# Branch taps as matmuls, one load per scan tile and step-size additions on ScalarE, in a four-layer kernel on one Trainium2 core

## The chip, the core and the metric

The kernel runs on one core of one Trainium2 chip, in one launch for a batch of eight images. The metric is the device time in microseconds (us), from the first to the last instruction and what little lies around them. All arithmetic is in 32-bit floats. The names of the engines in the profile are PE for TensorE (with PEld for its weight loads), DVE for VectorE, ACT for ScalarE, POOL for GpSimd, and SP for the engine that issues most of the DMAs; SPq and ACTq are the instruction queues of SP and ScalarE.

## The reference

Each image has 256 channels of 32 x 32 pixels, read as 1024 tokens. Four layers follow each other, each with a residual: attention over tokens, two 3x3 convolutions, and a large layer with a state-space scan ("mamba") on four groups of 64 channels, a gate, depthwise convolutions, a second attention and a projection. The change is in the scan of the last layer. Cut to that:

```
def mamba(xs, inw, convw, convb, xpw, dtw, dtb, alog, dp, outw):   # xs: tokens x 64
    xz = xs @ inw.T                                  # inw: 256 x 64
    u, z = jnp.split(xz, 2, axis=-1)                 # 128 channels each
    uc = causal depthwise convolution of u, 4 taps (convw), + convb
    u = silu(uc)
    xdbc = u @ xpw.T                                 # 4 + 16 + 16 columns
    dt = softplus(xdbc[..., :4] @ dtw.T + dtb)       # the step size
    Bm, Cm = xdbc[..., 4:20], xdbc[..., 20:]
    # scan over tokens, 128 channels x 16 states:
    #   h = exp(dt * A) * h + dt * u * Bm ;  y = sum over states of h * Cm
    y = selective_scan(u, dt, Bm, Cm, -exp(alog), dp)
    return y * silu(z) @ outw.T
```

## The kernel before

The program is written image by image, but it is not issued in that order. A recorder (class Plan) takes down every operation of all eight images, and a planner (arrange, L526) then writes the order of each engine by hand: it goes forward in time with a cost for each operation (cost, L329; matmul groups in appraise), and gives each engine the operation that can begin first. Among those that can begin equally soon it takes the one with the earliest due time. Due times come from the table PACE (L38): for every part and image four marks, between which the part's operations are spread. Only their order counts. The parts are A (first attention), O (its output projection), C (the two 3x3 convolutions), N (layer norm ahead of the scan), F0 to F3 (front of a branch), S (scan steps), Z0 to Z3 (back of a branch), B (gate, depthwise convolutions, second attention), E (the end), W and V (weights made once). The issue goes through one helper, so every line of the profile says L252; groups are told apart by tiles.

Each engine works off its order strictly one after another. So do the queues that issue DMAs: nearly all go through SP, and the weight chunks (chunk, L835; a ring of six tiles) through ScalarE's queue.

For every image there are four branches i, one for each group of 64 channels. branch_front (L1555) makes the scan's inputs:

- A matmul of 64 rows (the branch's channels in xn) by 128 columns (minw) into a two-bank PSUM tile, in two halves of 512 tokens; ScalarE copies the result into the single tile raw (L928), whose first three columns are zero.
- The four taps: ScalarE writes tap 3 with its bias into u, and VectorE adds the other three with three multiply-adds over 1024 columns. Tanh and one more VectorE step complete the silu. raw serves as scratch for the Tanh and again below.
- A small matmul makes Bm and Cm (low), which go to DRAM (bc). A second one makes the step size: VectorE adds dtb out of PSUM into a, ScalarE takes Abs and Exp, VectorE adds 1 into dt, and so on to the softplus. The step size dt and the product dt * u go to DRAM by store (L1547), ordered by channel group.

The scan (scan_steps, L1650) works on tiles of 128 partitions: 32 channels times four states. A scan tile therefore needs each row of dt and of dt * u four times (once for each state), and each row of bc 32 times. load_groups (L1665) and load (L1678) fetch these from DRAM with four DMAs each, one for every block of 32 partitions. For each of 64 units per image GpSimd multiplies (drive), and then twice ScalarE makes the decay into the only tile da in PSUM (decays) and VectorE scans (scan); VectorE multiplies by Cm (weigh), and TensorE sums over the four states with the 0/1 matrix sel (add_up, tile y). branch_back (L1625) uses the other 128 columns of minw for z.

conv_weights (L1406) prepares the weights of the two convolutions once, through the tiles room.

Of the kernel before, what the change touches and what calls it, by code (L numbers as in the profile page):

```python
# [20 lines left out]
P = 128  # L21
C = 256
# [17 lines left out]
        (-885, -784, -577, -524),  # L40
        (-103, -9, 78, 165),
        (485, 530, 588, 646),
        (870, 961, 1046, 1134),
        (1361, 1446, 1533, 1630),
        (1845, 1935, 2025, 2115),
        (2349, 2396, 2443, 2519),
        (2831, 2902, 2980, 3061),
    ),
    "B": (
        (1114, 1200, 1279, 1370),  # L50
        (1602, 1687, 1773, 1860),
        (2084, 2169, 2259, 2351),
        (2463, 2638, 2720, 2739),
        (3101, 3188, 3272, 3307),
        (3516, 3600, 3754, 3767),
        (3880, 3975, 4004, 4059),
        (4777, 4790, 5023, 5024),
    ),
    "C": (
        (-333, -53, 12, 184),  # L60
        (148, 323, 511, 689),
        (675, 782, 934, 1087),
        (1131, 1297, 1470, 1642),
        (1616, 1787, 1960, 2133),
        (2074, 2247, 2420, 2622),
        (2612, 2799, 2955, 3121),
        (3457, 3546, 3602, 3664),
    ),
    "E": (
        (1389, 1406, 1424, 1444),  # L70
        (1880, 1893, 2032, 2032),
        (2333, 2372, 2389, 2427),
        (2831, 2831, 2839, 2842),
        (3542, 3564, 3565, 3565),
        (3488, 3498, 3544, 3628),
        (3933, 3940, 3941, 4070),
        (4578, 4972, 4989, 5061),
    ),
    "F0": (
        (-559, -519, -387, -348),  # L80
        (363, 550, 550, 626),
        (1092, 1176, 1318, 1318),
        (1446, 1454, 1454, 1491),
        (1237, 1661, 1789, 1916),
        (1606, 1682, 1917, 1917),
        (2318, 2416, 2610, 2836),
        (2309, 2375, 2375, 2615),
    ),
    "F1": (
        (473, 510, 515, 531),  # L90
        (841, 1007, 1007, 1018),
        (1453, 1469, 1469, 1476),
        (1926, 2012, 2021, 2060),
        (2383, 2407, 2505, 2505),
        (2847, 2866, 2883, 2973),
        (2445, 2541, 2639, 2965),
        (3743, 3846, 3846, 3888),
    ),
    "F2": (
        (427, 665, 686, 726),  # L100
        (1098, 1110, 1122, 1137),
        (1591, 1596, 1608, 1621),
        (2148, 2148, 2150, 2159),
        (2673, 2691, 2758, 2758),
        (3061, 3062, 3062, 3067),
        (3456, 3471, 3476, 3483),
        (4079, 4079, 4079, 4079),
    ),
    "F3": (
        (741, 760, 761, 883),  # L110
        (1181, 1206, 1250, 1253),
        (1668, 1730, 1762, 1864),
        (2176, 2194, 2334, 2357),
        (2659, 2674, 2674, 2796),
        (3135, 3167, 3185, 3358),
        (3545, 3624, 3666, 3742),
        (4203, 4242, 4242, 4331),
    ),
    "N": (
        (228, 275, 297, 518),  # L120
        (894, 898, 916, 935),
        (1370, 1378, 1387, 1393),
        (1775, 1779, 1956, 1956),
        (2364, 2372, 2383, 2485),
        (2769, 2858, 2905, 2913),
        (3516, 3516, 3516, 3516),
        (3916, 3931, 3947, 3957),
    ),
    "O": (
        (-408, -360, -360, -222),  # L130
        (251, 266, 272, 304),
        (647, 699, 699, 717),
        (1141, 1144, 1164, 1169),
        (1628, 1641, 1641, 1653),
        (2121, 2128, 2128, 2130),
        (2664, 2673, 2673, 2673),
        (2983, 2987, 3029, 3137),
    ),
    "S": (
        (496, 662, 820, 969),  # L140
        (980, 1123, 1258, 1397),
        (1470, 1636, 1790, 1956),
        (1967, 2133, 2291, 2453),
        (2458, 2615, 2760, 2911),
        (2907, 3037, 3231, 3382),
        (3371, 3581, 3774, 3909),
        (3655, 3674, 4444, 4470),
    ),
    "V": (
        (-2135, -1874, -1869, -1869),  # L150
    ),
    "Z0": (
        (571, 587, 605, 700),
        (1086, 1087, 1087, 1125),
        (1562, 1567, 1573, 1651),
        (2046, 2046, 2067, 2274),
        (1457, 1941, 1964, 2015),
        (2915, 2931, 2940, 3087),
        (2942, 2968, 2993, 3076),
        (3891, 4014, 4213, 4213),  # L160
    ),
    "Z1": (
        (747, 752, 1035, 1038),
        (1215, 1215, 1215, 1325),
        (1653, 1666, 1667, 1787),
        (2101, 2105, 2228, 2271),
        (2632, 2641, 2641, 2719),
        (3117, 3172, 3218, 3304),
        (3106, 3600, 3605, 3608),
        (4127, 4151, 4151, 4159),  # L170
    ),
    "Z2": (
        (822, 833, 857, 967),
        (1360, 1394, 1403, 1429),
        (1878, 1878, 1905, 1931),
        (2340, 2377, 2377, 2392),
        (2686, 2778, 2788, 2829),
        (3276, 3276, 3399, 3482),
        (3695, 3695, 3735, 3945),
        (4495, 4548, 4753, 4758),  # L180
    ),
    "Z3": (
        (930, 938, 958, 959),
        (1442, 1444, 1445, 1457),
        (1878, 1881, 1882, 1883),
        (2411, 2421, 2447, 2452),
        (2890, 2903, 2904, 2905),
# [2140 lines left out]
```

## Time and profile before

| what | value |
| --- | --- |
| median of three runs | 5733.31 us (5718.4 to 5734.21) |
| the profiled execution | 5719.45 us, of which the span of its instructions is 5717.7 us |
| mean granted clock of TensorE in it | 0.898 of full speed |
| DMA moved | 553.96 MB, 97 GB/s on average |
| DMA issues for scan tiles (bc, dt, du) | 1024 + 512 + 512, each 128 KB |

The profile's groups show for each kind of instruction the engine, the tiles (out<-in, with buffer numbers left out), the shape, the count, then the busy time in us and the mean duration of one in ns, and last the idle time of the engine ahead of them with what ended it. A 512-column matmul of 32-bit floats appears as two records: the code issues 128 of them with minw, and the profile counts 256. In the table by stretches each row gives the length, then for each engine the busy time and number of instructions, then the granted clock of TensorE (PEclk), the share of DMA engines' time in use, and GB/s. Every number in this text that is called a share of the chain comes from the view that follows the work back from the last instruction.

### The profile page before, as it was taken

The page shows a single profiled execution, that of the slowest core. Times are in us where ns is not written, and L with a number is a line of the kernel's source. Part 1 is how long each engine was busy: PE and PEld are TensorE (multiplying, and loading weights), DVE is VectorE, ACT ScalarE, POOL GpSimd, SP SyncE. Part 2 cuts the span into 40 slices and gives each one's busy share as a digit, 9 for nine tenths or more (in the row PEclk, how much of TensorE's full clock was granted, in tenths as well). Part 3 has the DMA queues.
Part 4 walks back from the last instruction along what each step waited for, and adds up shares of the span by engine and source line. Part 5 has one row for each costly group of instructions (what it writes and reads, how often), then busy time and mean ns, then how long its engine had stood idle before and what let it go on. Part 6 is the DMA issues. An engine that isn't in the chain of part 4 may idle for free.

```text
span 5717.7 us, 56860 instructions
## 1 busy us (share of the span) xinstructions
PE 4851.9 (85%) x18854; PEld 1945.2 (34%) x18854; DVE 4044.5 (71%) x5285; ACT 2843.0 (50%) x3737; POOL 1309.9 (23%) x527
## 2 busy tenths in 40 slices
PE   8899898789799989999888998889889388587495
PEld 2343533432334333333333332333325033232132
DVE  3333667878866887687767686688866888688823
ACT  4343453456455646564555445465464345455242
POOL 0000123323320323112231123213240324133300
PEclk9999998899898999999899998889989589798597
DMA  3112434434342444324333334324433344233210
GB/s 121 55 55 74 127 84 127 130 99 116 110 120 65 122 120 125 87 79 124 111 96 92 96 98 115 85 78 121 120 101 91 89 127 117 60 112 109 60 34 23
DMA packets 267279, 553.96 MB, mean 97 GB/s; under 512 B 70616, under 2 KB 93784, under 8 KB 266976
## 3 DMA queue, kind: packets, MB, share of 16 engines
q1 hardware_dynamic: 182880, 413.89, 25.5%
q10 hardware_dynamic: 84096, 136.35, 8.2%
q8 instruction: 151, 2.47, 0.2%
q14 instruction: 152, 1.25, 0.1%
HBM read 478.98 MB, written 62.65 MB: 95 GB/s over the span
## 4 chain that ended last, share of the span: by engine, by line
PE 52%; DVE 22%; issue 9%; ACT 8%; DMA 7%; SPq 1%; POOL 1%; ACTq 0%; DVEq 0%; POOLq 0%
PE big L252 29%; PE cv L252 10%; PE acc L252 10%; DVE hs L252 10%; ACT p L252 3%; PE y L252 2%; DVE room L252 2%; ACT da L252 2%; DVE u L252 2%; DMA dt_m<-dt 1%; DMA du_m<-a 1%; DMA dt<-dt_m 1%; DVE fd L252 1%; SPq L252 1%; DMA bc<-bc 1%
## 5 line engine op out<-in xcount | busy, mean ns | idle before, releaser
L252 POOL TENSOR_TENSOR hs<-du,bc 128x1024 f32<-128x1024 f32 x512 | 1307.0, 2570 | 4069.7 <-PE y L252 1880.9
L252 ACT ACTIVATE p<-big 128x1024 f32<-128x1024 f32 x1024 | 1014.1, 1020 | 597.1 <-PE big L252 479.8
L252 ACT ACTIVATE da<-dt,a_neg 128x512 f32<-128x512 f32 x1024 | 708.0, 691 | 1044.8 <-DVE hs L252 814.8
L252 PE MATMUL acc<-p,v 128*64 128x512 f32 x3072 | 844.7, 634 | 82.1 <-ACT p L252 80.0
L252 PE MATMUL cv<-taps,w 128*128 128x256 f32 x3072 | 780.9, 405 | 90.2 <-DVE xt L252 30.4
L252 DVE TENSOR_TENSOR_SCAN hs<-da,carry,hs 128x512 f32<-128x512 f32 x512 | 653.6, 1276 | 199.1 <-ACT da L252 183.7
L252 DVE TENSOR_TENSOR_SCAN hs<-da,hs 128x512 f32<-128x512 f32 x512 | 623.2, 1217 | 236.6 <-ACT da L252 163.7
L252 DVE TENSOR_TENSOR hs<-hs,bc 128x1024 f32<-128x1024 f32 x512 | 725.9, 1421 | 64.3 <-ACT carry L252 59.4
L252 PEld LDWEIGHTS cv<-taps,w 128*128 128x128 f32 x3072 | 596.3, 201 | 367.6 <-issue 177.3
L252 PE MATMUL big<-q,k 64*128 64x512 f32 x2048 | 590.7, 652 | 40.5 <-ACT p L252 24.4
L252 DVE TENSOR_TENSOR p<-p 128x1024 f32<-128x1024 f32 x256 | 331.3, 1296 | 325.4 <-ACT p L252 194.1
L252 PE MATMUL y<-hs,sel 128*32 128x512 f32 x2048 | 372.6, 666 | 189.9 <-DVE hs L252 188.1
L252 PEld LDWEIGHTS acc<-p,v 128*64 128x64 f32 x3072 | 162.5, 138 | 671.5 <-issue 376.0
L252 PE MATMUL big<-qk,qk 32*128 32x512 f32 x2048 | 339.5, 691 | 36.7 <-DVE z L252 9.1
L252 PEld LDWEIGHTS big<-q,k 64*128 64x128 f32 x2048 | 161.3, 189 | 414.9 <-issue 215.4
L252 PE MATMUL cv<-p,v 128*64 128x512 f32 x1024 | 287.9, 640 | 3.2 <-DVE xt L252 3.2
L252 PE MATMUL big<-xn,w 128*128 128x512 f32 x512 | 231.4, 603 | 0.7 <-issue 0.6
L252 PE MATMUL big<-o,w 128*128 128x512 f32 x384 | 190.0, 644 | 44.0 <-DVE o L252 24.3
L252 PEld LDWEIGHTS y<-hs,sel 128*32 128x32 f32 x2048 | 54.9, 112 | 436.1 <-DVE hs L252 279.2
L252 PEld LDWEIGHTS big<-qk,qk 32*128 32x128 f32 x2048 | 93.3, 196 | 265.0 <-issue 169.5
L252 DVE SCALAR_TENSOR_TENSOR room<-room,vec,room 128x992 f32<-128x992 f32 (+1 forms) x128 | 165.5, 1293 | 12.7 <-ACT room L252 11.3
L252 PE MATMUL big<-fd,w 128*128 128x512 f32 x256 | 135.3, 681 | 43.6 <-DVE fd L252 31.9
(232 smaller groups left out, 5256.1 us busy)
## 6 DMA issues: line engine op xcount, KB each, us to landing
bc<-bc SPq DMA_DIRECT2D x1024, 128.0 KB
w<-wc ACTq DMA_DIRECT2D x384, 256.0 KB
dt<-dt_m SPq DMA_DIRECT2D x512, 128.0 KB
du<-du_m SPq DMA_DIRECT2D x512, 128.0 KB
rs<-inv SPq DMA_DIRECT2D x64, 256.0 KB
dt_m<-dt SPq DMA_DIRECT2D x64, 256.0 KB
du_m<-a SPq DMA_DIRECT2D x64, 256.0 KB
w<-in_wqk ACTq DMA_DIRECT2D x64, 128.0 KB
```

The costliest lines, as they stand in the source:

```text
L252: made = op["call"](*args, **kwargs).ins
```

## The change

Seven edits are made together:

1. The four taps go into the projection's weights. front_weights makes, once, four scaled copies of each branch's 64 x 128 weights (one for each tap), transposes them on TensorE and stores them in DRAM as two 128-row matrices per branch (wu). In branch_front two DMAs put the branch's 64 rows of xn twice into raw, into partitions 64 to 127 one column later than into 0 to 63, and four 512-column matmuls of 128 rows (two per half, accumulating) give the result of all four taps. ScalarE moves it from PSUM to u with the bias. The copy into raw and the three multiply-adds are gone.
2. The weights wu are fetched as a chunk for each branch, in the ring of six; minw keeps only the columns for z.
3. A scan tile's partitions are ordered by channel first and state second (sel, by_state), and dt, dt * u and bc are each loaded by one DMA of 128 partitions instead of four of 32.
4. The two additions of the step size (dtb, and 1) are Identity activations on ScalarE, no longer VectorE instructions.
5. All due times in PACE are new.
6. region (the planner's view of an access) counts several partition dimensions; the cost of a large memset is raised from 0.3 to 0.83 ns an element.
7. front_weights runs as the last piece of part V.

```diff
--- before.py
+++ after.py
@@ -37,167 +37,167 @@
 PACE = {
...
     "C": (
...
-        (2612, 2799, 2955, 3121),
-        (3457, 3546, 3602, 3664),
...
+        (3483, 3656, 3824, 3986),
+        (4157, 4407, 4623, 4825),
     ),
...
     "S": (
...
-        (3371, 3581, 3774, 3909),
-        (3655, 3674, 4444, 4470),
...
+        (4582, 4689, 4769, 4839),
+        (5152, 5207, 5207, 5581),
     ),
     "V": (
-        (-2135, -1874, -1869, -1869),
+        (306, 325, 327, 412),
     ),
...
@@ -297,8 +297,8 @@
         return a.tensor.name, 0, 1, a.offset, a.offset + sum((n - 1) * s for s, n in ap)
     row = int(np.prod(a.tensor.shape[1:]))
     p, at = divmod(a.offset, row)
-    end = p + (ap[0][1] - 1) * max(1, ap[0][0] // row) + 1
-    return a.tensor.name, p, end, at, at + sum((n - 1) * s for s, n in ap[1:])
+    end = p + sum((n - 1) * (s // row) for s, n in ap if s >= row) + 1
+    return a.tensor.name, p, end, at, at + sum((n - 1) * s for s, n in ap if s < row)
 
 
 def whole_banks(r):
@@ -344,7 +344,7 @@
         return (334 if e == 2 else 420), first
     if e == 1:
         if name == "memset":
-            took = 60 + 0.3 * n
+            took = 60 + (0.83 if n > P else 0.3) * n
         elif name == "tensor_tensor_scan":
             took = 70 + 2.3 * n
         elif name == "reciprocal":
@@ -858,9 +858,17 @@
     make_identity(nc, ident)
 
     sel = wp.tile([P, 32], F32, name="sel")
-    for s in range(4):
-        rows = slice(s * 32, s * 32 + 32)
-        vector.tensor_copy(sel[rows], ident[rows, rows])
+    pool.memset(sel, 1.0)
+    for base, sign in ((0, 1), (3, -1)):
+        pool.affine_select(
+            out=sel,
+            in_=sel,
+            compare_op=ALU.is_ge,
+            fill=0.0,
+            base=base,
+            pattern=[[-4 * sign, 32]],
+            channel_multiplier=sign,
+        )
 
     gmat = wp.tile([P, P], F32, name="gmat")
     pool.memset(gmat, 0.125)
@@ -905,6 +913,7 @@
     made_w = {"fcw": fc_w}
     for name in ("wc1", "wc2"):
         made_w[name] = wdp.tile([12, P, 4, P], F32, tag=name, name=name)
+    made_w["wu"] = wdp.tile([NB, P, 2, P], F32, tag="wu", name="wu")
     minus_s1 = wp.tile([P, 2], F32, name="minus_s1")
     vector.tensor_scalar_mul(minus_s1, vec[:, cols["s1"] : cols["s1"] + 2], -1.0)
     q_b = wp.tile([P, 2], F32, name="q_b")
@@ -1427,6 +1436,32 @@
             for k in range(2):
                 sync.dma_start(out=outer_w[:, :, k], in_=w[:, :, 2 * k])
 
+    def front_weights():
+
+        w = room[0][:, 0:C].rearrange("p (i n) -> p i n", i=NB)
+        sync.dma_start(out=w, in_=I["wu"])
+        scaled = room[2].rearrange("p (i k n) -> p i k n", i=NB, k=4)
+        ps = big_tile()
+        for i in range(NB):
+            for k in range(4):
+                vector.tensor_scalar(
+                    scaled[:, i, k], w[:, i], col("convw", 4 * i + 3 - k), None, ALU.mult
+                )
+            for k in range(2):
+                at = (2 * i + k) * P
+                tensor.matmul(
+                    ps[:, at : at + P],
+                    room[2][:, at : at + P],
+                    ident,
+                    start=True,
+                    stop=True,
+                )
+        vector.tensor_copy(room[2], ps)
+        sync.dma_start(
+            out=made_w["wu"].rearrange("i p k n -> p i (k n)"),
+            in_=room[2].rearrange("p (i n) -> p i n", i=NB),
+        )
+
     def transform(xt, stats, h):
 
         scale, shift = stats
@@ -1556,29 +1591,21 @@
 
 
         j, rows = i // 2, slice((i % 2) * 64, (i % 2) * 64 + 64)
-        ps = big_tile()
+        for half, at in ((slice(0, 64), 2), (slice(64, P), 3)):
+            sync.dma_start(out=raw[half, at : at + N], in_=inner(xn[j])[rows])
+        w, ps = chunk("wu", i), big_tile()
         for h in range(2):
-            tensor.matmul(
-                ps[:, HALVES[h]],
-                minw[rows, j, 0:P],
-                inner(xn[j])[rows, HALVES[h]],
-                start=True,
-                stop=True,
-            )
-        scalar.copy(raw[:, 3 : 3 + N], ps)
+            for k in range(2):
+                tensor.matmul(
+                    ps[:, HALVES[h]],
+                    w[:, k],
+                    raw[:, 2 - 2 * k + h * HALF : 2 - 2 * k + (h + 1) * HALF],
+                    start=k == 0,
+                    stop=k == 1,
+                )
         u = mp.tile([P, N], F32, tag="u", name="u", bufs=2)
         uu = u[:, 0:N]
-        scalar.activation(
-            uu,
-            raw[:, 3 : 3 + N],
-            AF.Identity,
-            bias=col("convb", i),
-            scale=col("convw", 4 * i + 3),
-        )
-        for k in range(3):
-            vector.scalar_tensor_tensor(
-                uu, raw[:, k : k + N], col("convw", 4 * i + k), uu, ALU.mult, ALU.add
-            )
+        scalar.activation(uu, ps, AF.Identity, bias=col("convb", i))
         th = raw[:, 3 : 3 + N]
         scalar.activation(th, uu, AF.Tanh, scale=0.5)
         vector.scalar_tensor_tensor(uu, th, 1.0, uu, ALU.add, ALU.mult)
@@ -1610,10 +1637,10 @@
             tensor.matmul(
                 ps[:, HALVES[h]], mdtw[:, i], u[:, HALVES[h]], start=True, stop=True
             )
-        vector.tensor_scalar_add(aa, ps, col("dtb", i))
+        scalar.activation(aa, ps, AF.Identity, bias=col("dtb", i))
         scalar.activation(ee, aa, AF.Abs)
         scalar.activation(ee, ee, AF.Exp, scale=-1.0)
-        vector.tensor_scalar_add(dd, ee, 1.0)
+        scalar.activation(dd, ee, AF.Identity, bias=ones[:, 0:1])
         vector.scalar_tensor_tensor(ee, dd, -1.0, ee, ALU.add, ALU.subtract)
         scalar.activation(dd, dd, AF.Ln)
         vector.tensor_sub(dd, dd, ee)
@@ -1629,7 +1656,7 @@
         for h in range(2):
             tensor.matmul(
                 ps[:, HALVES[h]],
-                minw[rows, j, P : 2 * P],
+                minw[rows, j],
                 inner(xn[j])[rows, HALVES[h]],
                 start=True,
                 stop=True,
@@ -1667,11 +1694,10 @@
             if u["q"] == 0:
                 t = dtp.tile([P, 2, HALF], F32, tag=name, name=name)
                 src = br[name][:, u["h"], g : g + 2].rearrange("d g n -> d (g n)")
-                for s in range(4):
-                    sync.dma_start(
-                        out=t[s * 32 : s * 32 + 32].rearrange("d g n -> d (g n)"),
-                        in_=src,
-                    )
+                sync.dma_start(
+                    out=t.rearrange("p g n -> p (g n)"),
+                    in_=src.unsqueeze(1).to_broadcast([32, 4, 2 * HALF]),
+                )
                 br[name, u["gp"]] = t
             u[name] = br[name, u["gp"]]
 
@@ -1682,11 +1708,10 @@
                 t = bcp.tile([P, 2, HALF], F32, tag="bc", name="bc")
                 src = br["bc"][4 * u["q"] : 4 * u["q"] + 4, u["h"]]
                 src = src.rearrange("s k n -> s (k n)")
-                for s in range(4):
-                    sync.dma_start(
-                        out=t[s * 32 : s * 32 + 32].rearrange("d k n -> d (k n)"),
-                        in_=src[s : s + 1].to_broadcast([32, 2 * HALF]),
-                    )
+                sync.dma_start(
+                    out=t.rearrange("p k n -> p (k n)"),
+                    in_=src.unsqueeze(0).to_broadcast([32, 4, 2 * HALF]),
+                )
                 br["bc", u["q"]] = t
             u["bc"] = br["bc", u["q"]]
 
@@ -2176,6 +2201,7 @@
     with plan.part("V", 0):
         conv_weights("wc1")
         conv_weights("wc2")
+        front_weights()
     for b, img in enumerate(imgs):
         with plan.part("A", b):
             front_attention(image_of(b), img)
@@ -2239,7 +2265,7 @@
     def by_state(v):
 
         v = v.reshape(NB, 4, 32, 4, 4)
-        return v.transpose(4, 2, 0, 3, 1).reshape(P, -1)
+        return v.transpose(2, 4, 0, 3, 1).reshape(P, -1)
 
     def by_output(w):
 
@@ -2286,8 +2312,9 @@
         "wc1": conv_w(a["L1_conv_quant_weights"]),
         "wc2": conv_w(a["L2_conv_kernel"]),
 
+        "wu": c(w3("m_inw")[:, :P].transpose(1, 0, 2)),
         "minw": c(
-            w3("m_inw").reshape(2, 2, 256, DM).transpose(1, 3, 0, 2).reshape(P, 2, 256)
+            w3("m_inw")[:, P:].reshape(2, 2, P, DM).transpose(1, 3, 0, 2).reshape(P, 2, P)
         ),
         "mxpw": c(w3("m_xpw")[:, DTR:].transpose(2, 0, 1)),
         "mxdt": c(w3("m_xpw")[:, :DTR].transpose(1, 0, 2)),
```

## The prediction

> **What bounds the kernel now.** I read the page first: how busy each engine is, and how that runs over the span.
>
> ```profile
> PE 4851.9 (85%) x18854; PEld 1945.2 (34%) x18854; DVE 4044.5 (71%) x5285; ACT 2843.0 (50%) x3737; POOL 1309.9 (23%) x527
> ...
> PE   8899898789799989999888998889889388587495
> ...
> DVE  3333667878866887687767686688866888688823
> ...
> PE 52%; DVE 22%; issue 9%; ACT 8%; DMA 7%; SPq 1%; POOL 1%; ACTq 0%; DVEq 0%; POOLq 0%
> ```
>
> TensorE is busiest and has half of the chain, but its row falls to 3, 5, 7 and 4 near the end, where VectorE's row stays at 8. So I cut the span into four stages: until the first branch, the long middle, the last two images' scans, and what follows the last scan (columns as in the section on the profile).
>
> ```profile
> 0.00:572.00 572.00, 524.57 (x2009) 211.08 (x2009) 204.84 (x510) 224.04 (x277) 2.92 (x15) 0.96 0.25 76
> 572.00:4433.00 3861.00, 3437.74 (x13517) 1403.33 (x13517) 2936.55 (x3825) 2046.57 (x2736) 987.61 (x389) 0.92 0.37 105
> 4433.00:5434.00 1001.00, 682.10 (x2520) 250.25 (x2521) 826.40 (x834) 469.00 (x621) 319.42 (x123) 0.77 0.34 97
> 5434.00:5718.00 284.00, 207.48 (x812) 80.56 (x810) 76.67 (x119) 103.37 (x104) 0.00 (x0) 0.84 0.08 26
> ```
>
> In the middle TensorE is 89% busy (3438 of 3861), VectorE 76%. In the third stage VectorE is at 83%, TensorE at 68% and at a granted clock of only 0.77. The waits of TensorE in that third stage say for whom:
>
> ```profile
> PE y L252 <- DVE hs L252: 157.4, 40, 9.1
> PE big L252 <- DVE u L252: 58.5, 5, 27.6
> PE acc L252 <- ACT p L252: 22.1, 30, 3.5
> ```
>
> With the smaller entries of that list, 264 of its 319 us of idle time end on VectorE. In the middle it is about 211 of 423 us. So the kernel is bound by TensorE in the middle, and by VectorE's scans at the end.
>
> **The change part by part.** The rows that I cost it from:
>
> ```profile
> L252 PE MATMUL big<-xn,w 128*128 128x512 f32 x512 | 231.4, 603 | 0.7 <-issue 0.6 <-DVE z L252 0.2
> L252 PE MATMUL big<-xm,w_minw 64*128 64x512 f32 x256 | 140.8, 670 | 5.8 <-DVE ln_r L252 2.7 <-ACT xm L252 1.6 <-DVE xm L252 0.9
> L252 DVE SCALAR_TENSOR_TENSOR u<-raw,vec,u 128x1024 f32<-128x1024 f32 x96 | 131.5, 1370 | 4.2 <-ACT u L252 3.5
> L252 DVE TENSOR_SCALAR a<-big,vec 128x1024 f32<-128x1024 f32 x32 | 40.8, 1276 | 27.7 <-PE big L252 17.7 <-DMA du_m<-a 7.1 <-DMA du<-du_m 2.6
> L252 DVE TENSOR_SCALAR dt<-raw 128x1024 f32<-128x1024 f32 x32 | 26.4, 825 | 3.5 <-ACT raw L252 3.4
> L252 ACT ACTIVATE qk<-big,vec 128x1024 f32<-128x1024 f32 x16 | 17.7, 1105 | 8.8 <-PE big L252 8.8
> L252 ACT ACTIVATE fd<-xs,vec 128x1024 f32<-128x1024 f32 x16 | 19.8, 1237 | 0.3
> ```
>
> *VectorE* loses 131.5 us of taps and 40.8 + 26.4 us of additions: 198.7 us, 5% of its work. By the share of the tile raw's VectorE time in each stage (224.5 us in the middle, 61.2 us in the third), 156 us of it lie in the middle and 43 us in the third.
>
> *ScalarE* loses the copy into raw (32.3 us) and gets two additions: 32 x 1.105 us out of PSUM (nearest row: qk) and 32 x 1.237 us in SBUF (nearest row: fd). The step into u now reads PSUM, 1.105 instead of 1.24 us. The sum is +39 us, 50 to 51% busy. The Trainium skill ("ScalarE: Activation LUTs", Rules for kernel authors) says to keep additions on VectorE. The rows agree on the durations: 2.34 us per branch on ScalarE against 2.10 us on VectorE, so by the rule the move loses 32 x 0.24 = 8 us. But VectorE is the one that ends the waits, and an idle half of ScalarE hides it; I take 0, and +8 if that cover is gone.
>
> *TensorE*: half of the minw records go, 128 x 0.55 us = 70.4 us (140.8 / 256 each). In come 32 x 4 matmuls of 128 rows, 256 records; the row xn streams them at 231.4 / 512 = 0.452 us, so 115.7 us. That is +45.3 us: 36 in the middle, 9 in the third stage. The skill ("TensorE: Matmul & The Clock Gate", Why this matters for your kernels) says that a matmul on few rows takes as long as one on 128 and gains only from others beside it. By that rule the old records would have cost 57.9 us and the difference would be +58. The rows show that the lone 64-row ones are dearer, so I keep 45.
>
> *What this makes of the stages.* In the middle the +36 us stand on the bound. Against it, VectorE's free time grows from 924 to 1080 us, 17%; if TensorE's 211 us of waits for it shrink by as much, 36 us come back (ends: 0, and 156). Sum 0. In the third stage the ends are 0 and 43 us; I take 30, near the upper one, because VectorE is 83% busy and ends five sixths of the waits. TensorE's 9 us there mostly fall into its 319 idle us: +3.
>
> *Loads.* SP issues 2048 loads for scan tiles at 0.42 us (median) = 860 us. After it 512 at about 0.38 us (the 512 KB loads of 128 rows, xs and xm, take 0.37 to 0.38) = 195 us. What the queue does at a branch start:
>
> ```profile
> 4953.28 2.63 SPq L252 DMA_DIRECT2D dt<-dt_m  x4
> 4956.59 9.15 SPq L252 DMA_DIRECT2D du<-du_m  x8
> 4965.78 1.81 SPq L252 DMA_DIRECT2D dt<-dt_m  x4
> ```
>
> Sixteen loads, 2 MB, take 14.3 us to issue, 147 GB/s, with the DMA engines half in use (0.50 and 0.57 in these stretches), while they reach 239 GB/s just after. At that rate the same 2 MB take 8.8 us, 38% less. The chain has dt_m, du_m, dt and bc DMAs for 4.3%, 246 us; 38% of it is 94 us. The lower end is 0 (no run shows a load whose source repeats each row four times; it could also be slower by as much as the two-dimensional stores, 0.57 us to issue, 512 x 0.19 = 97 us of SP, which has that time). I take a third of the upper end, -30: most loads run ahead, and the bytes stay.
>
> *The new DMAs and waits.* Each branch gets two 256 KB loads into raw, on SP. They wait for the last reader of raw in the branch before (the subtraction of its softplus). Behind them in SP's queue stand stores and scan loads, for which GpSimd and ScalarE wait; behind the projection on TensorE stand attention and convolution matmuls. In the trace of the first image, raw is free at 626.2 us and the taps are done at 635.6: 9.4 us for copy, tap and three multiply-adds. In the new order it is issue 0.4 + landing about 2.6 (the last load of the batch above: 2.56 us) + eight records 3.6 + ScalarE 1.1 = 7.7 us. The branch itself isn't later even when nothing hides the load. The cost is TensorE standing still for it: between 0 and 32 x 3.0 = 96 us. I take +5, because branches other than the first two of an image are 100 us apart and the order puts the load ahead. The 32 weight loads of 128 KB on ScalarE's queue (0.33 us each to issue, 11 us) lie in its idle half: 0, up to +11.
>
> *Weights once*: 16 VectorE scalings of 256 columns (row of that size: 0.29 us), one copy of 1.2 us, eight 128-column transposes, 16 records x 0.16 us = 2.6 us. They fall into stage one, where VectorE is 36% busy and TensorE 92%: +3 (0 to +10). The matrix sel is built in the same idle time: 0.
>
> *The new due times* have no row. They put the last image's convolutions across the scan of the image before (marks 4157 to 4825 against 4582 to 4839) where they ended before its middle (3457 to 3664 against 3371 to 3909), so TensorE keeps some of its convolution work (781 us for eight images, 98 each) for the stretch in which it lacks any. Bounds: -98 and, if the order fits worse, +80 (a quarter of the third stage's idle time). I take -15.
>
> Sum: 0 - 30 + 3 - 30 + 5 + 3 - 15 = -64 us. The profiled execution took 5719.45 us (span 5717.7, 1.75 around it), so 5655. The median of the three runs is 13.9 us above it: 5669, say 5670, 1.1% less.
>
> **The rivals.** (a) *The order at the end decides.* The third stage has 319 us of idle TensorE and a clock of 0.77. If the new order covers 100 us more of it than I took, the time is 5570. For it: the row of digits; against it: marks are ranks, and the planner's costs aren't the chip's. (b) *It cancels.* TensorE's +45 and the waits saved offset each other, and the loads are hidden: 5720 to 5750. For it: TensorE's half of the chain. (c) *Slower: TensorE waits in line for raw.* Its order is fixed, so a projection that reaches the head before its load has landed stops attention too, and at a granted clock that fell to 0.50 in such gaps. With 3.0 us per branch, 96 us, plus 45, less the 30 of the third stage: 5733 + 111 = 5845. It decides once the wait exceeds 64 / 32 = 2.0 us per branch on top of what I took. For it: SP's own waits, 1003 us on VectorE's scans alone, can hold the load back; against it: 100 us between branches. (d) *One load isn't faster than four*, since the bytes are the same: then my -30 is gone, 5700.
>
> **How the numbers follow.** A measurement of this kernel can tell about 0.3%, 17 us, from no change. Chances: my sum, with (d) as its upper part, 0.45 (5600 to 5710, likeliest 5670); (a) 0.17 (5500 to 5600); (b) 0.10 (5716 to 5750); (c) 0.28 (5751 to 5860). Faster is 0.62, same 0.10, slower 0.28. The range 5550 to 5800 leaves out about half of (a) and of (c).
>
> **What would show it.** Right: VectorE near 3850 us busy, ScalarE near 2880, TensorE near 4900; no u<-raw,vec group; waits of TensorE for u and hs shorter in the scans of the last images; SP issuing 1500 fewer DMAs, and GpSimd starting sooner after a store. Wrong: a group of projection matmuls with over 60 us of idle time ended by a DMA into raw; TensorE's busy time over 4950; the scans' third stage as long as before.

## The result: 0.3% slower, where 1.1% faster was forecast

| kernel | median, us | ratio to before, 95% interval | in us of 5718 |
| --- | --- | --- | --- |
| before | 5717.76 (20 runs) | 1 | |
| after | 5736.71 (5706.23 to 5768.19, 20 runs) | 1.0033 [1.0017, 1.0048] | +19 (10 to 27) |

The sign is the other one. The profiled execution of after has a span of 5733.5 us, 15.8 more than before's, at a mean granted clock of 0.916 (before 0.898), so the clock isn't what it lost by. The page first (busy time by engine, then the 40 slices of TensorE and VectorE):

```profile
PE 4885.0 (85%) x18998; PEld 1957.5 (34%) x18998; DVE 3929.1 (69%) x5138; ACT 2874.1 (50%) x3768; POOL 1305.7 (23%) x530
...
PE   8999997788889898899889898978888788777595
...
DVE  3334488678767787657866887668867878678823
```

TensorE gained 33 us of busy time and VectorE lost 115 (the forecast had 45 and 199). The 3 and the 5 near the end of TensorE's row are both 7 now, but of the slices ahead of them more lost a tenth than gained one. The same by stages, cut at the same times:

```profile
0.00:572.00 572.00, 534.76 (x2047) 216.64 (x2048) 211.49 (x561) 229.50 (x286) 3.31 (x18) 0.98 0.26 77
572.00:4433.00 3861.00, 3379.81 (x13287) 1354.34 (x13285) 2844.01 (x3602) 2041.14 (x2729) 1000.30 (x395) 0.93 0.35 108
4433.00:5434.00 1001.00, 749.44 (x2808) 298.04 (x2805) 792.30 (x842) 493.40 (x643) 302.09 (x118) 0.84 0.33 103
5434.00:5734.00 300.00, 220.97 (x863) 88.50 (x861) 81.27 (x135) 110.10 (x110) 0.00 (x0) 0.85 0.09 29
```

TensorE's idle time in the third stage fell from 319 to 252 us, and in the middle it rose from 423 to 481. Over the whole span TensorE is 33 us busier and 17 us less idle; by the forecast's sum the idle time had to fall by about 109. Yet the last scan begins its last product (the one with Cm, on VectorE) at 5410 us (before 5407), and what follows takes 323 us (before 311). The waits of TensorE show the exchange. First the third stage of after:

```profile
PE y L252 <- DVE hs L252: 83.1, 20, 11.0
...
PE acc L252 <- ACT p L252: 23.2, 32, 2.8
PE big L252 <- DVE u L252: 20.4, 6, 7.2
```

The wait for the scans halved there (157.4 before), and that for u fell from 58.5. Then the middle, 572 to 4433 us, of before:

```profile
PE acc L252 <- ACT p L252: 51.3, 74, 4.0
PE big L252 <- ACT p L252: 34.2, 23, 6.2
PE y L252 <- DVE hs L252: 30.8, 15, 5.2
```

and the same stretch of after:

```profile
PE y L252 <- DVE hs L252: 96.2, 33, 10.9
PE acc L252 <- ACT p L252: 66.9, 70, 9.4
PE big L252 <- ACT p L252: 56.1, 49, 7.2
```

The 74 us that the third stage no longer waits for the scans are back in the middle as 65. The convolutions are what moved: of the busy time of their PSUM tile cv, 828 us lay in the middle and 122 in the third stage before, 765 and 168 after. That fits: the work that fills TensorE's holes was carried from one place to another, and the middle lost what had covered its scans and its attention. Adding up the whole list of TensorE's waits by who ended them gives, before and after: VectorE 574 and 526 us, ScalarE 201 and 259, no visible cause 61 and 22, DMA 18 and 25.

The 12 us behind the last scan have a cause of their own. These are the multiply-adds of the last depthwise convolution that VectorE still has to do there, before (5407 us to the end) and after (5411 us to the end):

```profile
L252 DVE SCALAR_TENSOR_TENSOR room<-room,vec,room 128x992 f32<-128x992 f32 (+1 forms) x21 | 26.0, 1236 | 5.6 <-ACT room L252 5.0
L252 DVE SCALAR_TENSOR_TENSOR room<-room,vec,room 128x992 f32<-128x992 f32 (+1 forms) x29 | 35.8, 1235 | 7.2 <-ACT room L252 6.4
```

Both kernels have 128 of them; in the new order eight more, 10 us, stand behind the scans, and TensorE's wait for room in that stretch goes from 31.7 to 44.8 us. In all traces here the two go together: with 16 to 21 of them behind the last scan what follows takes 307 to 315 us, with 29 of them 323 to 328.

The rows that the change touched, in after (groups as in the prediction):

```profile
L252 PE MATMUL big<-raw,w 128*128 128x512 f32 x256 | 123.2, 622 | 12.8 <-DMA raw<-xm 10.2 <-ACT p L252 1.2 <-ACT v L252 1.1
L252 PE MATMUL big<-xm,w_minw 64*128 64x512 f32 x128 | 65.5, 645 | 10.7 <-DVE room L252 7.3 <-ACT qk L252 2.0 <-ACT low L252 0.9
L252 DVE SCALAR_TENSOR_TENSOR u<-raw,u 128x1024 f32<-128x1024 f32 x32 | 47.0, 1467 | 39.5 <-ACT raw L252 36.7 <-DMA dt<-dt_m 2.8
L252 ACT ACTIVATE dt<-raw,ones 128x1024 f32<-128x1024 f32 x32 | 36.7, 1148 | 23.7 <-DVE u L252 19.6 <-PE da L252 2.8 <-PE cv L252 1.2
L252 ACT ACTIVATE u<-big,vec 128x1024 f32<-128x1024 f32 x32 | 35.6, 1111 | 89.4 <-PE big L252 89.3
L252 ACT ACTIVATE a<-big,vec 128x1024 f32<-128x1024 f32 x32 | 35.4, 1107 | 32.8 <-PE big L252 27.3 <-DMA du_m<-a 5.5
```

The fold's matmuls cost 123 us (115.7 forecast) and wait 10 us for raw. Each of these rows costs what was forecast for it, within 8 us, but for u<-raw,u, which was 1257 ns before. The view of the chain in after covers only a few per cent of the span and can't be used.

### The profile page after: what moved, and what is told of

It reads as the page before. It is cut to its first block, busy times and chain, and to the rows that moved or that the text cites. A ratio compares the mean times of both kernels' runs of the same rounds, so it can differ in the third digit from the quotient of the medians.

```text
span 5733.5 us, 54648 instructions
## 1 busy us (share of the span) xinstructions
PE 4885.0 (85%) x18998; PEld 1957.5 (34%) x18998; DVE 3929.1 (69%) x5138; ACT 2874.1 (50%) x3768; POOL 1305.7 (23%) x530
## 5 line engine op out<-in xcount | busy, mean ns | idle before, releaser
L252 PE MATMUL cv<-taps,w 128*128 128x256 f32 x3072 | 766.2, 399 | 49.1 <-issue 20.2
L252 DVE TENSOR_TENSOR hs<-hs,bc 128x1024 f32<-128x1024 f32 x512 | 709.0, 1388 | 53.7 <-ACT carry L252 47.9
L252 ACT COPY carry<-hs 128x2 f32<-128x2 f32 x256 | 49.5, 194 | 209.0 <-DVE hs L252 167.6
```

Of the source, the lines that this page charges most:

```text
L252: made = op["call"](*args, **kwargs).ins
```

## The experiments

Two theories stood against each other at first. A: the edits gain about what was forecast where the order is kept, and the new order takes it back. B: TensorE's own work sets the time, so relief of VectorE buys next to nothing and the extra matmuls are paid in full. To tell edits from order, most kernels here are changed *in place*: the planner plans the operations of the kernel that they are made from, and where an edit applies, other instructions are issued at the places of the planned ones. So every engine keeps its order apart from the edited instructions. It is one addition to Plan.issue:

```diff
-            made = op["call"](*args, **kwargs).ins
+            now = op.get("now", [(op["engine"], op["call"], args, kwargs)])
+            for engine, call, args, kwargs in now:
+                made = call(*args, **kwargs).ins
```

plan.instead(back, ...) fills "now" of an operation that was just recorded. Differences are given in us of 5718; against after they are the difference of two ratios to before, 1.0033 being that of after, with some 10 to 15 us of uncertainty.

### The edits in before's order

*The additions on ScalarE* (e3).

```diff
         vector.tensor_scalar_add(aa, ps, col("dtb", i))
+        plan.instead(1, (scalar, "activation", (aa, ps, AF.Identity), {"bias": col("dtb", i)}))
...
         vector.tensor_scalar_add(dd, ee, 1.0)
+        plan.instead(1, (scalar, "activation", (dd, ee, AF.Identity), {"bias": ones[:, 0:1]}))
```

> The kernel before with its due times and the order of every engine kept; only the two step-size additions of each branch are issued on ScalarE at the places where VectorE had them (VectorE -67 us, ScalarE +71 us). Theory A (the edits gain where the order is kept, and the new order of after takes the gain back): 10 to 40 us less than before. Theory B (TensorE's own work sets the time, relief of VectorE buys next to nothing): within 10 us of before. If ScalarE's idle half does not cover the move: 10 us or more above.

Measured 5711.63 us, ratio 0.9982 [0.9972, 0.9991]: -10 us. The gain is at the edge of both theories, and doesn't tell them apart; ScalarE's idle half does cover the move.

*The multiply-adds left out* (e4).

```diff
             vector.scalar_tensor_tensor(
                 uu, raw[:, k : k + N], col("convw", 4 * i + k), uu, ALU.mult, ALU.add
             )
+            plan.instead(1)
```

> The kernel before in its order, without the three VectorE multiply-adds of each branch: three of the four taps are not computed, everything else is. VectorE -131 us, TensorE unchanged: the most that the fold of the taps can gain by relief of VectorE. Theory A: 40 to 100 us less than before (the 30 us of the third stage and some in the middle). Theory B: at most 20 us less.

Measured 5685.89 us, 0.9938 [0.9924, 0.9952]: -35 us, between the two: more than B allows, less than A expected. 131 us less VectorE work buy 35.

*The projection twice* (e5).

```diff
+            again = ((ps[:, HALVES[h]], minw[rows, j, 0:P], inner(xn[j])[rows, HALVES[h]]),
+                     {"start": True, "stop": True})
+            plan.instead(1, (tensor, "matmul", *again), (tensor, "matmul", *again))
```

> The kernel before in its order, with each branch's projection matmul for u issued twice (64 more matmuls, 128 records of 0.55 us, TensorE +70 us; the second repeats the first and changes nothing of what is computed). The price of more TensorE work by itself, where the fold adds 45 to 53. Theory A (TensorE has idle time that takes half of it): +15 to +40 us. Theory B (TensorE sets the time): +60 to +75 us.

Measured 5740.18 us, 1.0036 [1.0023, 1.0048]: +21 us. The minw row grew by 59 us of busy time and TensorE's whole busy time by 42, so a third to a half of new TensorE work is paid. The fold's 45 us would cost 16 to 22 at that price (an estimate). B falls: TensorE's work isn't paid in full.

*One load for four* (e6).

```diff
                 for s in range(4):
                     sync.dma_start(out=t[s * 32 : s * 32 + 32].rearrange("d g n -> d (g n)"), in_=src)
+                    one = {"out": t.rearrange("p g n -> p (g n)"),
+                           "in_": src.unsqueeze(1).to_broadcast([32, 4, 2 * HALF])}
+                    plan.instead(1, *[(sync, "dma_start", (), one)] * (s == 3))
```

(the same for bc, with the partition order of after)

> The kernel before in its order, with one load for the four quarter-loads of each scan tile, issued where the last of the four was, and the partition order that goes with it (SP 2048 scan loads to 512). Theory A: 20 to 50 us less than before, the forecast's -30. Theory B, and the rival in which one load is no faster than four: within 8 us. If the load whose source repeats each row is slower than four plain ones: 10 to 40 us more.

Measured 5699.26 us, 0.9963 [0.9951, 0.9975]: -21 us. The forecast's term (-30) holds in this order, at two thirds of its size.

*Additions and loads together* (b1: e3 and e6 in one kernel).

> The kernel before in its own order, with the two edits that gained there, the additions on ScalarE and the single loads, and nothing else. If the gains add up: 5718 - 10 - 21, about 5688 us, less than both kernels. If the second takes the place of the first (both only move the start of VectorE's scans): 5695 to 5700.

Measured 5703.33 us, 0.9976 [0.9968, 0.9985]: -14 us. The gains don't add: b1 isn't better than the loads alone, and 3 us above what was expected if the second only takes the place of the first. It is less than both kernels, as e6 is.

So in before's order the edits are worth -10 - 35 + 16 - 21 = -50 us if they added; by b1 (-14 for -31) -33, and with the dearer price of TensorE's work -27. The fold as a whole wasn't run in before's order: its part of this sum is put together from e4 and e5.

### The order

*The edits undone in after's order* (a1 to a4): the same method the other way round. Shown is the fold, whose matmuls become one of 64 rows for each half, and whose ScalarE step becomes the copy, the first tap and three multiply-adds. Here minw keeps its columns for z, and those for u get a tile of their own, minu; what prepares wu stays in.

```diff
         scalar.activation(uu, ps, AF.Identity, bias=col("convb", i))
+        plan.instead(1,
+            (scalar, "copy", (raw[:, 3 : 3 + N], ps), {}),
+            (scalar, "activation", (uu, raw[:, 3 : 3 + N], AF.Identity),
+             {"bias": col("convb", i), "scale": col("convw", 4 * i + 3)}),
+            *[(vector, "scalar_tensor_tensor",
+               (uu, raw[:, k : k + N], col("convw", 4 * i + k), uu, ALU.mult, ALU.add), {})
+              for k in range(3)])
```

> The kernel after with its due times and the order of every engine kept, with the fold of the taps undone in place: one 64-row projection matmul per half, copy into raw, first tap and three multiply-adds where the fold's ScalarE step stands; no loads into raw and of wu. VectorE +131 us, TensorE -53 us. Against after: theory A (the fold gains in a kept order) +15 to +60 us; theory B (TensorE sets the time, and the fold costs its 45 to 53 us) -20 to -50 us.

Measured 5875.31 us, 1.0287 [1.0264, 1.0310]: +145 on after, far over both. Much of it can be the place where the multiply-adds had to go: VectorE stood 68 us in front of them for ScalarE's step (3.5 us in before).

```profile
L254 DVE SCALAR_TENSOR_TENSOR u<-raw,vec,u 128x1024 f32<-128x1024 f32 x96 | 143.7, 1496 | 70.2 <-ACT u L254 67.7
```

So a1 is no price of the fold.

> The kernel after in its order, with four quarter-loads of 32 partitions again for each scan tile, at the place of the one load, and the old partition order. Against after: theory A +20 to +50 us; theory B, or one load no faster than four, within 8 us; one load slower than four: 10 to 40 us less.

Measured 5707.54 us, 0.9984 [0.9975, 0.9993]: 28 us *less* than after. The same edit gains in one order and loses in the other.

> The kernel after in its order, with the two step-size additions on VectorE again in place. VectorE +67 us, ScalarE -72 us. Against after: theory A +10 to +40 us; theory B within 10 us; if the move cost ScalarE's path: less than after by up to 10 us.

Measured 5760.06 us, 1.0081 [1.0060, 1.0101]: +27 on after, as A had it.

> The kernel after in its order, with the fold, the loads and the additions all undone in place: the work of before in the order and by the due times of after. It is the price of the order alone. Theory A (edits gain about 60 us in a kept order, the new order loses about 80): 5770 to 5830 us. Theory B (the order is worth little or a small gain, the 45 to 53 us of TensorE work are what is paid): 5680 to 5700 us.

Measured 5857.12 us, 1.0248 [1.0224, 1.0272]: the work of before costs 142 us more in after's order than in its own, more than A had expected. That is too much for a price of the order: this order was planned for a front without multiply-adds, and three of them are forced into it, as in a1.

*The new due times for the old work* (e1: before with after's PACE, and the order planned anew).

```diff
-PACE = {...}   # of before
+PACE = {...}   # of after
```

> The kernel before, its work unchanged, with the due times of after: every engine's order is planned anew for the old work. Theory A (the order that these due times give is the worse one, for TensorE's waits for ScalarE and for the tail): 30 to 100 us more than before, 5750 to 5820 us. Theory C (the order is as good as the old one, and after loses by the load's and VectorE's own behaviour): within 15 us of before.

Measured 5935.15 us, 1.0388 [1.0373, 1.0402]: +222 us, a multiple of what A expected. Due times that serve one kernel are bad for another with nearly the same work. But it is no more than random moves of before's own due times cost (below, +269 and +343), so it doesn't show that after's due times are worse than others that weren't chosen for this work. The other pair, after's work with before's due times, wasn't run.

*How much any order matters*: each row of the due times moved by one random number from -3 to 3 us, the work unchanged (two rows of jb_jitter_4):

```diff
-        (-885, -784, -577, -524),
-        (-103, -9, 78, 165),
+        (-887, -786, -579, -526),
+        (-104, -10, 77, 164),
```

> The kernel after, its work unchanged, each row of its due times moved by up to 3 us at random, so that the order is planned anew. If the order's chance is small: within 10 us of after. If the due times of after are a found best: 20 to 150 us more.

> The kernel after, work unchanged, due times moved by another random draw of up to 3 us. If the first draw (+94 us on after) was typical: 50 to 250 us more than after. If it was unlucky: within 30 us of after.

> The kernel before, its work unchanged, each row of its due times moved by up to 3 us at random. If the order's chance is small: within 10 us of before. If the due times of before are a found best: 20 to 150 us more.

> The kernel before, work unchanged, due times moved by another random draw of up to 3 us. If the first draw (+270 us on before) was typical: 50 to 300 us more than before. If it was unlucky: within 30 us of before.

| draw | median, us | ratio to before | against its own kernel, us |
| --- | --- | --- | --- |
| ja_jitter_6 (work of after) | 5831.05 | 1.0182 [1.0160, 1.0204] | +85 |
| ja_jitter_3 (work of after) | 5870.11 | 1.0262 [1.0242, 1.0282] | +131 |
| jb_jitter_4 (work of before) | 5992.21 | 1.0470 [1.0451, 1.0490] | +269 |
| jb_jitter_2 (work of before) | 6059.47 | 1.0599 [1.0575, 1.0623] | +343 |

All four draws lose, and the two of before's work by more than was expected of each. What is lost shows in TensorE's waits, whose list begins so in before and in jb_jitter_4:

```profile
PE y L252 <- DVE hs L252: 188.1, 55, 9.1
...
PE y L252 <- DVE hs L252: 325.8, 83, 16.2
PE acc L252 <- ACT p L252: 88.6, 129, 5.9
```

With nothing changed but ranks, TensorE waits 138 us more to sum over states, and everything behind those sums in its order stands. So one choice of ranks is worth several times what all the edits are, and the 19 us between the kernels lie far within that. Both draws of after's work are also faster than both of before's, by 122 to 228 us: each kernel has due times that suit it, before's more so, and a comparison of the two kernels compares those as well. Two draws of each are too few to give this a size.

### Why single loads lose in the new order

VectorE is 56 us less busy with the loads undone than in after, though it does the same work (its page line in a2):

```profile
PE 4875.5 (85%) x18998; PEld 1956.4 (34%) x18998; DVE 3873.5 (68%) x5142; ACT 2873.2 (50%) x3768; POOL 1305.0 (23%) x527
```

The collision theory: a VectorE instruction gets longer while GpSimd's product (hs<-du,bc) runs, and single loads move those products to where VectorE has other work. An estimate from the records of the traces: taking the shortest tenth of each VectorE group as its undisturbed time, what instructions beside a running product take above that is about 260 us in before, 308 in after and 248 in a2 (how the groups are cut moves all three together by up to 30, the steps between them by less than 10). The test is to double the product (p3).

```diff
             pool.tensor_mul(u["hs"], u["du"], both_groups(u["bc"][:, 0]))
+            again = (pool, "tensor_mul", (u["hs"], u["du"], both_groups(u["bc"][:, 0])), {})
+            plan.instead(1, again, again)
```

> The kernel after in its order, with GpSimd's product of each scan unit issued twice (the second repeats the first; GpSimd 1306 to about 2610 us, half its time still idle, and the products end a median of 14 us before their scans). Collision theory: VectorE's instructions beside it get longer, its busy time rises by 150 to 300 us with no instruction added, and the time by about half of that, 75 to 150 us. If GpSimd's running doesn't lengthen VectorE's instructions: VectorE's busy time within 30 us of after, the time within 30 us.

Measured 6258.25 us, 1.0940 [1.0919, 1.0961]: +519 us on after, several times what was expected. VectorE is 543 us busier with no instruction added, and idle for about as long (1804 us in after, 1784 in p3). Which rows grew tells how; first after:

```profile
L252 DVE TENSOR_TENSOR hs<-hs,bc 128x1024 f32<-128x1024 f32 x512 | 709.0, 1388 | 53.7 <-ACT carry L252 47.9 <-DMA du<-du_m 1.5
L252 DVE TENSOR_TENSOR_SCAN hs<-da,hs 128x512 f32<-128x512 f32 x512 | 623.0, 1217 | 259.6 <-ACT da L252 226.2 <-POOL hs L252 32.2
...
L252 DVE SCALAR_TENSOR_TENSOR z<-z,big 128x1024 f32<-128x1024 f32 x32 | 38.8, 1214 | 27.7 <-ACT z L252 27.7
```

and p3:

```profile
L254 POOL TENSOR_TENSOR hs<-du,bc 128x1024 f32<-128x1024 f32 x1024 | 2757.1, 2706 | 3150.4 <-DMA du<-du_m 1353.2 <-PE y L254 1140.9 <-DVE norm L254 159.3
L254 DVE TENSOR_TENSOR hs<-hs,bc 128x1024 f32<-128x1024 f32 x512 | 916.2, 1792 | 56.7 <-ACT carry L254 52.6
...
L254 DVE TENSOR_TENSOR_SCAN hs<-da,hs 128x512 f32<-128x512 f32 x512 | 622.5, 1216 | 265.8 <-ACT da L254 179.9 <-POOL hs L254 74.7 <-issue 9.0
...
L254 DVE SCALAR_TENSOR_TENSOR z<-z,big 128x1024 f32<-128x1024 f32 x32 | 38.6, 1207 | 25.0 <-ACT z L254 25.0
```

The product with both operands in SBUF (hs<-hs,bc) went from 1388 to 1792 ns; the scan and z<-z,big, which take one operand from PSUM (da, big), didn't move. Matched row by row, the rows with an operand in PSUM make -1 us of the 543 and the rest all of it. It is the rule of the Trainium skill ("SBUF — State Buffer", Who interferes with whom): a VectorE instruction with two SBUF inputs contends with a GpSimd instruction that reads SBUF, and one with at most one SBUF input doesn't, outside the 2-port modes. The runs agree on both halves; the exception of the 2-port modes is not tested here. The doubled product also ends later: VectorE's scans wait for it 141 us instead of 52, far less than the 519.

Which loads matter? With the loads of GpSimd's inputs made four again in after's order (q2; one load of 128 partitions becomes four of 32, in the new partition order), and with dt alone made four (q3):

```diff
+FOUR = ("du", "bc")      # q3: ("dt",)
...
+                if name in FOUR:
+                    plan.instead(1, *[(sync, "dma_start", (), one) for one in four])
```

> The kernel after in its order and with its partition order; dt keeps one load, dt * u and bc (the two inputs of GpSimd's product) are loaded by four again. Undoing all three gave 29 us less than after. If single loads cost because GpSimd's product starts earlier and runs beside VectorE's other instructions (collision theory): most of the 29 us come back, 15 to 30 us less than after, and VectorE's busy time falls by 30 to 56 us. If the partition order or the load of dt is what costs: within 8 us of after.

> The kernel after in its order and with its partition order; dt * u and bc keep one load, dt is loaded by four again (ScalarE waits for it, GpSimd doesn't). Collision theory: within 8 us of after, VectorE's busy time within 15 us. If it is the load of dt that costs: 15 to 30 us less than after.

q2: 5712.42 us, 0.9991 [0.9983, 0.9999], 24 less than after, VectorE busy 3872.1, 57 less. q3: 5726.98 us, 1.0017 [1.0008, 1.0026], 9 less, which can't be told from 0 (the intervals overlap), VectorE 24 less, somewhat more than expected. So the partition order isn't the cause, and most of the loss sits in GpSimd's two inputs, as the theory has it. (In q2 the loads are not those of before: a quarter that repeats its rows takes 644 ns to issue, a plain one 419.) The same in before's order, dt alone by one load (c1):

```diff
+                    now = [one] * (s == 3) if name == "dt" else [quarter]
+                    plan.instead(1, *[(sync, "dma_start", (), x) for x in now])
```

> The kernel before in its order, with the new partition order, dt loaded by one DMA, dt * u and bc by four as before. All three single gave 21 us less than before. Collision theory (singles for GpSimd's inputs cost, the single for dt gains): 20 to 40 us less than before, VectorE's busy time no higher than before's 4045. If what gains is the number of DMAs that SP issues: a quarter of the issues are saved, 5 to 10 us less.

Measured 5704.92 us, 0.9969 [0.9956, 0.9981]: -18 us, just short of what was expected, VectorE busy 4047.0. That is no better than all three (-21, VectorE 4070.1). In this order the gain comes with the load of dt, and the 26 us by which VectorE is busier in e6 cost nothing that can be measured.

The rival is that the loads lose because they change when the scan's inputs land. VectorE's wait for GpSimd's product, in after and in a2, speaks against it:

```profile
DVE hs L252 <- POOL hs L252: 51.6, 13, 10.3
DVE hs L254 <- POOL hs L254: 79.1, 19, 13.5
```

With the loads undone VectorE waits 27 us longer for the products, and the kernel is still 28 us faster. What got better is the length of its instructions: matched row by row, -59 us in rows with no operand in PSUM and +1 in those with one. That lengthening beside GpSimd is real and can set the time is shown (p3); that it is why the loads of du and bc lose in the new order fits q2 and a2 in both columns, but no run changes the lengthening alone, so it stays the likely cause.

## Why the prediction was wrong, by its own steps

The miss is 83 us: -64 was forecast, +19 measured. Two terms of the sum failed, the new due times and the loads, and they hang together, as the loads change sign with the order.

- **The new due times, -15.** This step failed. The two bounds were -98 and +80, and it came out near the upper one: the edits are worth -27 to -50 in before's order, and the result is +19, so the new order costs +46 to +69 against before's, with what it makes of the loads counted in. This is a difference, not a run. Two marks of it are the same in after and in all kernels that undo edits in its order: TensorE waits 256 to 277 us for ScalarE (178 to 201 in before and the kernels in its order), and from the last product of the scans to the end it takes 323 to 328 us (309 to 313), for the eight multiply-adds more that stand there. The forecast saw rightly that convolutions would move into the third stage (its idle time fell by 67 us), and counted this as gain; it didn't ask what the middle (idle +58) and the end would lose. The filling work itself (cv) stayed as it was, 1082 and 1068 us in all.
- **Loads, -30.** This step failed too, in the order that was built: right in before's order (-21), wrong in sign there (+28 against undoing them). That alone is 58 of the 83 us: with the loads undone (a2) the new order's kernel is 9 us under before, where the forecast without its loads is 34 under. The loss that the term allowed for was a slower issue; that a scan tile that lands sooner could cost time was not in it. SP's part is as the forecast had it, roughly: 512 issues take 269 us (by medians, 519 ns the load of dt, 536 du, 524 bc) where 195 were reckoned and 2048 took 860. At a branch start of the last image the queue now does this:

```profile
4962.82 1.30 SPq L252 DMA_DIRECT2D dt<-dt_m  x2
4964.18 1.26 SPq L252 DMA_DIRECT2D du<-du_m  x2
```

  Four loads are issued in 2.6 us, where sixteen took 14.3. But GpSimd was seldom the one waited for, as its products end a median of 13 us before their scans in before and 14 in after; VectorE's waits for them fell by 31 us (83.0 to 51.6), and what starting them sooner likely did besides was to put them beside other VectorE work.
- **VectorE's relief, -36 in the middle and -30 in the third stage.** The work left (198.7 us), but VectorE's busy time fell by 115: the rows that both kernels have got 62 us longer, matched one by one, all of it in rows with no operand in PSUM (by the estimate above about 48 us beside a running product), the new weights take 5, and the rest isn't assigned. The forecast priced VectorE's rows as if a row had one duration; u<-raw,u went from 1257 to 1467 ns. What relief is worth was near: e4 gives 35 us for 131, where 66 for 199 were reckoned.
- **TensorE +36 and +3, less 36.** The size was near: by its rows +48, in TensorE's whole busy time +33. The price is a third to a half of the work (e5), near what the forecast had for the third stage; for the middle it had taken all of it against waits for VectorE that would shrink by as much. Those waits didn't shrink: in the list of the middle they go from 232 us (the forecast read 211) to 263.
- **Waiting for raw, +5.** 10.2 us. Rival (c), TensorE in line for raw, is out. ScalarE +39 measured as +31, weights once +3: not separated. Slips that don't matter: the scalings of the weights have 64 columns, not 256 (16 of 0.25 us), ScalarE's own numbers sum to +38, and rival (c)'s to 5844.
- **Rivals.** (b), it cancels, is what the time says (5720 to 5750), but not by its mechanism: TensorE's extra work takes back a third to a half of what it was to take, and the order, with what it makes of the loads, takes the rest. (d), one load no faster than four, was nearer than the forecast in the order that counts, where one load is the slower. (a) was right that the order decides and wrong in sign: the third stage did get less idle, and the scans ended as late as before, one of the forecast's own signs of being wrong.

## What to carry to other kernels

Where the order is planned for the whole program, price an edit in the frozen order first, and count a new order as a term of its own, which here was about as large as all edits together, or larger; an edit's price can change its sign with it. Moving filling work into a hole can open one where it came from: read the waits of both stretches before counting the gain. Before starting a transfer earlier, ask what will then run beside the work that it releases.

## What the runs showed of the hardware that was not expected

- VectorE's instructions on two SBUF operands are longer beside GpSimd's product: hs<-hs,bc 1388 ns on average with one product a unit, 1792 with two; the scans and z<-z,big, with an operand in PSUM, stay within 1%. With products doubled, each us that VectorE got busier cost 0.96 us of time (519 for 543), though VectorE was idle for 29% of the span. That ratio is of two totals; no run shows it for a single instruction.
- Moving due times by up to 3 us costs 85 to 343 us, and the granted clock changes with the order alone (0.898 in before, 0.884 in jb_jitter_4).
- One load whose source repeats each row four times takes 519 to 536 ns to issue, a plain quarter of it 419: 128 partitions at once aren't four times dearer, only 1.25 times. A quarter whose source also repeats its rows (q2) takes 644, more than the whole.
